# Attention with a key search, experts and a local mixer on one core: small search updates moved to GpSimd, whose instructions then stand in written order

## The chip, the core and the metric

The kernel runs on one core of a Trainium2 chip. A core has five engines that work side by side and wait for each other through semaphores: TensorE (PE in the profile, with its weight loads as PEld), VectorE (DVE), ScalarE (ACT), GpSimd (POOL) and SyncE (SP, here only a queue for DMAs). Each engine takes its instructions in a fixed order: an instruction that waits holds up all that stand behind it on its engine. DMAs move data between DRAM and on-chip memory; SP, ACT and GpSimd issue them, and such an issue is an instruction in that engine's order.

The metric is device time in microseconds (us) of one execution.

## What is computed

Two layers on a batch of 4 images of 32 x 32 tokens with 384 channels. Layer 0 is an attention with a search for important keys, followed by a mixture of 4 experts with the best 2 per token; layer 1 is a local attention over 3 x 3 neighbours and a feed-forward layer. The change touches layer 0:

```python
attn = softmax(einsum('bhnd,bhmd->bhnm', q, k) * scale)
gidx = argmax(einsum('bhnd,hgd->bhng', q, gp), axis=-1)      # 48 groups
q_mean = mean of the q of each group
qmw_t = einsum('bhgd,bhnd->bhgn', q_mean, k)
_, tidx = top_k(qmw_t, 96)                                   # of 1024 keys
col = how often each key was taken, over the groups
attn = attn * row[..., :, None] * col[..., None, :]
attn = attn / (attn.sum(axis=2, keepdims=True) + 1e-08)      # over queries
out = einsum('bhnm,bhmd->bhnd', attn, v) ; x = x + out @ proj_w.T
# experts
probs = softmax(layernorm(x) @ gate_w + gate_b); keep the best two
x = x + sum_e share_e * (gelu(layernorm(x) @ w1[e] + b1[e]) @ w2[e] + b2[e])
```

## The kernel before

**Attention as a pipeline of steps.** There are 48 heads (4 images of 12). A head's 1024 x 1024 scores are done in 4 steps of two 128-key blocks, so there are 192 steps and some more to drain. All instructions are written in one loop, and what is written in a step is spread over time by offsets:

- `scores(u)`: 8 matmuls (L649) into two PSUM buffers; `exps` (L659): two exponentials on ACT that empty them into `e` tiles. The next step's scores need these two buffers back.
- `total`, one step later: 8 matmuls with ones (L667, ps_z) that add up the exponentials by query. After a head's fourth step `gather` copies the sums (ACT, zr, L681) and sends them through DRAM with two DMAs on SP (z_row, zz); `spread` adds and inverts them on DVE (L693, L695) and broadcasts them with two more (r_row, rz).
- `share`, 7 steps after the scores: on DVE, multiplies e by rz (L711, two a step) with a sum by key, and scales v by the inverse (wv, L716, L718).
- `out`, 8 steps after the scores: 8 matmuls (L667, ps_o) of e by wv. After a head's last one `keep` copies the result (po, L731, ACT) and writes it over the head's rows of q: two plain DMAs on SP (L740), then two accumulating DMAs on GpSimd (L738) that add the odd blocks and wait for the plain ones to land.
- Each head works on rows of q and k laid out four times over the partitions (`q4`, `k4`): eight DMAs on GpSimd (L636, L637), written where the head before begins.

**The search** (`topk`) works on tiles of 128 rows of `qmw_t`, 20 tiles in all, at most two at a time. It bisects: ACT counts with a Sign and an accumulator how many of 1024 values are above a bound (L391, into the scratch `junk`), two small DVE instructions on 128 x 1 (L395, L397) make the next bound, and so eight times over; L387 makes the first bound, L401 the edge. Then DVE picks the last candidates (L404, L407 and a chain of small ones to L424), and ACT counts once more (L429). `search()` moves every active search on by one piece and is called twice a step, with `end()` between, so that a Sign and its update stand a step apart. `junk` is the same memory as `below`, which DVE uses in L404.

**Other work in the steps.** A list of units with costs fills TensorE: transposes, q, k and v of the next image, group means, and for the image before, `project` (output projection) with `residue` loading x for it into `o` (one buffer), and `routed`: gate, the best two experts, and 16 indirect DMAs on GpSimd (L1400, two per token tile, four a step) that write token numbers into a table in DRAM by slot.

**Experts.** `experts` runs 35 blocks of 256 slots (three of 128). For each it gathers 2.4 MB of `up` and 2.6 MB of `down` (L1603), slot numbers `ids` (L1617) and token rows `xb` (L1627) with indirect DMAs on GpSimd, double-buffered. The last image's projection, its routing, and `schedule` (which blocks go to which expert, with the running sums `rt_start`) are done beside the first blocks; `add` gathers the two results of a token (`yt`, L1567) when both are there.

**What sets the order.** Attention and experts stand in one region in which the order of PE, DVE, ACT and SP is as written. GpSimd isn't in that list: a scheduler places its instructions, earlier than written where their inputs allow. So the first blocks' weights are issued among the last heads' row loads, and all of a head's eight row loads follow each other.

Of the kernel before, what the change touches and what calls it, by code (L numbers as in the profile page):

```python
# [10 lines left out]
FP = mybir.dt.float32  # L11
BF = mybir.dt.bfloat16
AF = mybir.ActivationFunctionType
ALU = mybir.AluOpType
# [3 lines left out]
P = 128  # L18
B, IMG, C = 4, 32, 384
NTOK = IMG * IMG  # L20
NB = NTOK // P
# [16 lines left out]
FIRST_BOUND, NEAR, SLOPE = 1.65, 92, 0.00366  # L38
# [138 lines left out]
def attention(net, outer, router, x, x1, unsafe, qkv_wT, gpT, proj_wT, proj_w, gate_w, gate_b):  # L177
# [24 lines left out]
    with ExitStack() as ctx:  # L202
# [71 lines left out]
        nc.gpsimd.memset(topped[:, 0, :], 1.0)  # L274
        nc.gpsimd.memset(topped[:, 1, :], float(2 * TOPK - NTOK))
        below = const.tile([P, 512], FP, name="below")
        junk = below.bitcast(mybir.dt.bfloat16)
        fit = const.tile([P, B], FP, name="fit")
        onehot = const.tile([P, B * KC * NB // 2], FP, name="onehot")
        sums = lasting.tile([P, NE], FP, name="sums")  # L280
# [83 lines left out]
        def topk(b, t):  # L364
# [19 lines left out]
            nc.scalar.activation(junk[:n], left[:n], AF.Abs, accum_out=size[:n])  # L384
            yield
            bound = small("tk_bound")
            nc.vector.tensor_scalar(bound[:n], size[:n], -FIRST_BOUND / NTOK, None, ALU.mult)  # L387
            for turn in range(len(DAMP) + 1):
                yield
                over = small("tk_over")  # L390
                nc.scalar.activation(junk[:n], left[:n], AF.Sign, bias=bound[:n], accum_out=over[:n])  # L391
                yield
                if turn == len(DAMP):
                    break
                nc.vector.scalar_tensor_tensor(step[:n], over[:n], float(NTOK - 2 * NEAR), size[:n], ALU.add, ALU.mult)  # L395
                old, bound = bound, small("tk_bound")
                nc.vector.scalar_tensor_tensor(  # L397
                    bound[:n], step[:n], -SLOPE * DAMP[turn] / NTOK, old[:n], ALU.mult, ALU.add
                )
            edge = best[:, 0:1]  # L400
            nc.vector.tensor_scalar(edge[:n], bound[:n], -1.0, None, ALU.mult)  # L401
            for half in range(2):
                cols = slice(half * 512, half * 512 + 512)
                nc.vector.scalar_tensor_tensor(  # L404
# [216 lines left out]
        class Head:  # L621
            def __init__(self, n):
                self.n, self.b, self.h = n, n // NH, n % NH
                self.c, self.j = self.h // 4, self.h % 4
                self.rows = slice(32 * self.j, 32 * self.j + 32)
                self.im = images[self.b]
                assert (self.b, self.c, "qk") in reached

                self.q4 = big.tile([P, 512], FP, name="q4", tag="q4", bufs=2)
                self.k4 = big.tile([P, 512], FP, name="k4", tag="k4", bufs=2)  # L630
                q = self.im["q"][self.c][self.rows, :]
                k = self.im["k"][self.c][self.rows, :].rearrange("p (a e t) -> p a e t", e=2, t=P)
                for r in range(4):
                    rows_ = slice(32 * r, 32 * r + 32)
                    odd, half = divmod(r, 2)
                    nc.gpsimd.dma_start(out=self.q4[rows_, :], in_=q[:, 512 * half : 512 * half + 512])  # L636
                    nc.gpsimd.dma_start(  # L637
                        out=self.k4[rows_, :].rearrange("p (a t) -> p a t", t=P), in_=k[:, :, odd, :]
                    )
                self.es = []  # L640
                self.s = tiny.tile([P, NB], FP, name="s", tag="s")

            def scores(self, u):
                self.ps = []
# [8 lines left out]
                        )  # L653
                    self.ps.append(ps)

            def exps(self):
                for ps in self.ps:
                    e = ep.tile([P, NTOK], FP, name="e", tag="e")
                    nc.scalar.activation(e, ps, AF.Exp, bias=shift, scale=QK_SCALE)  # L659
                    self.es.append(e)  # L660
# [12 lines left out]
            def total(self, u):  # L673
                if u == 0:
                    self.z = ps_z.tile([P, 512], FP, name="ps_z", tag="z")
                self.four(self.z, u, lambda odd: ones)

            def gather(self):

                zr = work.tile([P, 512], FP, name="zr", tag="zr", bufs=1)  # L680
                nc.scalar.copy(zr, self.z)  # L681
                there = rows.tile([4, 512], FP, name="z_row", tag="z_row")
                nc.sync.dma_start(out=there, in_=zr.rearrange("(j r) q -> j r q", r=32)[:, 0, :])
                self.zz = tiny.tile([P, 2, NB], FP, name="zz", tag="zz", bufs=2)
                nc.sync.dma_start(
                    out=self.zz,
                    in_=there.rearrange("j q -> (j q)").rearrange("(e p i) -> p e i", e=2, p=P),
                )
# [68 lines left out]
        def residue(b, t):  # L757
            if late:
                o = late[0].tile([P, C], FP, name="o", tag="o", bufs=2)
            else:  # L760
                o = few.tile([P, C], FP, name="o", tag="o", bufs=1)
            residues[b, t] = o
            r = b * NTOK + t * P
            nc.sync.dma_start(out=o, in_=x[r : r + P, :])
# [81 lines left out]
        def search():  # L846

            for one in list(searching):
                if next(one, 0) == 0:
                    searching.remove(one)  # L850
# [25 lines left out]
        for step in range(-AHEAD, 0):  # L876
# [8 lines left out]
                search()  # L885
            end()
        heads.append(Head(0))
        goal = spent
        for step in range(STEPS + OUT + 2):
            n, u = divmod(step, PAIRS)  # L890
            if n < NHEAD:
                heads[n].scores(u)
            if n < NHEAD:
                heads[n].exps()
            if 0 <= step - OUT < STEPS:
                heads[(step - OUT) // PAIRS].out((step - OUT) % PAIRS)
            if 0 <= step - 1 < STEPS:
                heads[(step - 1) // PAIRS].total((step - 1) % PAIRS)
            if u == 0 and 0 < n <= NHEAD:
                heads[n - 1].gather()  # L900
            if u == 0 and n + 1 < NHEAD:
                heads.append(Head(n + 1))
            if 0 <= step - OUT < STEPS:
                if (step - OUT) % PAIRS == PAIRS - 1:
                    heads[(step - OUT) // PAIRS].keep()
            b, i = divmod(step, PAIRS * NH)
            goal = min(goal + (RAMP if step < 12 else PACE), spent + MOST)
            begin(step)
            if step < 12:
                search()  # L910
                search()
            widen(step)
            o, t = i - OUT - 2, (i - OUT - 2) // 2
            if b and 0 <= o < 2 * NB and o % 2 == 0:
                project(b - 1, t)
            if b and o > 2 * NB:
                next(routing[b - 1], None)
            if b < B:
                for t in {3: [0], 4: [1, 2], 5: [3], 6: [4], 7: [5, 6], 8: [7]}.get(i, []):
                    value(b, t)  # L920
            while spent < goal and prepared():
                pass
            if zeros and step >= 4:
                zeros.pop(0)()
            if 0 <= step - SHARE < STEPS:
                heads[(step - SHARE) // PAIRS].share((step - SHARE) % PAIRS)
            if u == 1 and 0 < n <= NHEAD:
                heads[n - 1].spread()
            if b and 0 <= o + 1 < 2 * NB and o % 2:
                residue(b - 1, t + 1)  # L930
            search()
            end()
            search()
        residue(B - 1, 0)
        assert not ends and not others
        assert pending == [None, None] and begun == len(tiles) and not searching and not zeros
# [304 lines left out]
class Router:  # L1241
# [10 lines left out]
    def __init__(self, net, pool, keep, psum):  # L1252
# [4 lines left out]
        def const(name, shape, dtype=FP):  # L1257
            return pool.tile(shape, dtype, name=f"rt_{name}")
# [38 lines left out]
        nc.gpsimd.memset(self.upto[:, 0, :], 0.0)  # L1297
        self.index = [keep.tile([P, NT], mybir.dt.int32, name=f"index_{n}", tag=f"index_{n}") for n in range(2)]
        self.weight = [keep.tile([P, NT], FP, name=f"weight_{n}", tag=f"weight_{n}") for n in range(2)]
        none = const("none", [P, self.LINE], mybir.dt.int32)  # L1300
        nc.gpsimd.memset(none, 0)
        n = NE * NT
# [10 lines left out]
    def route(self, b, logit, mean, rs):  # L1313
# [82 lines left out]
        for t in range(NB):  # L1396
            if t % 2 == 0:
                yield
            for n in range(2):
                s = nc.gpsimd.indirect_dma_start(  # L1400
                    out=self.net.table, out_offset=bass.IndirectOffsetOnAxis(ap=there[n][:, t : t + 1], axis=0),
                    in_=ids[:, t, :], in_offset=None,
                )
                for o in sent:
                    self.tc.declare_no_dep(s.ins, o, reason="slots of tokens are distinct")
                sent.append(s.ins)
# [920 lines left out]
def metaformer_kernel(  # L2327
# [58 lines left out]
    with ExitStack() as outer:  # L2386
        router = routing(outer)
        eng = mybir.EngineType
        with tc.manual_schedule(engines={eng.PE, eng.DVE, eng.Activation, eng.SP}):
            left = attention(  # L2390
                net, outer, router, x, x1, unsafe, qkv_wT, gpT, proj_wT, proj_w, gate_w, gate_b
            )
            done = experts(net, router, x1, x2, wup, wdown, left)
# [75 lines left out]
```

## Time and profile before

| what | value |
|---|---|
| median of 3 runs (lowest, highest) | 2760.5 us (2757.79, 2776.32) |
| the profiled execution, its span | 2739.55 us, 2737.4 us |
| mean granted clock of TensorE | 0.964 of full |
| busy: PE, DVE, ACT, POOL | 93%, 64%, 46%, 23% |
| first scores of the loop; last ps_o of attention | 80.1 us; 1195.3 us |
| first expert matmul (L1723) | 1198.45 us |
| exponential L659; share L711; Sign L391 | 1107 ns x384; 1275 ns x384; 1151 ns x160 |
| updates L395, L397 | 146 ns, 158 ns, x140 each |
| row loads L636, L637; accumulating stores L738; tables L1400 (on GpSimd) | 512, 657; 885; 1120 ns |

Attention takes about 1100 us, the experts about 985, layer 1 about 557. A profile is one execution; the timed runs lie a little above it. In the answers quoted below, a row of waits gives who waited, for what, and then the sum in us, how many times, and the longest. A row of the timeline gives the start and the length in us, the engine, the source line, the operation, out<-in, and in brackets the idle time before it and what ended it.

### The profile page before, as it was taken

What the parts mean: (1) busy time and instruction counts of PE and PEld (TensorE: products, weight loads), DVE (VectorE), ACT (ScalarE), POOL (GpSimd) and SP (SyncE); (2) the same over time, 40 slices, a digit from 0 to 9 for tenths busy, and PEclk for the clock granted to TensorE, in tenths of its full rate; (3) what the DMA queues carried; (4) which work ended last, traced back from release to release, by engine and by line L of the source; (5) the groups of instructions that cost most, each with busy time, mean ns of one, the idle gap of its engine ahead of it and who ended that gap; (6) DMA issues with size and microseconds to landing.
All of it is one profiled execution on the core that took longest, in us unless ns stands there. A gap on an engine that the chain in (4) does not pass through costs nothing. (4 is left out here: it accounts for less than half of the span.)

```text
span 2737.4 us, 40223 instructions
## 1 busy us (share of the span) xinstructions
PE 2541.4 (93%) x14667; PEld 1549.7 (57%) x14667; DVE 1746.2 (64%) x4490; ACT 1270.0 (46%) x2086; POOL 635.3 (23%) x909
## 2 busy tenths in 40 slices
PE   6979998989899998779999999999999999999988
PEld 3323332333233332248889999999899984555532
DVE  2367768777788778756434454554555468888962
ACT  3768876768677876512122112112111223545455
POOL 2112322252225222613221112222222121210000
PEclk9989999999999998979999999999999999999989
DMA  5133434422332233444574554666566546765532
GB/s 110 38 98 90 105 92 120 106 61 62 83 89 62 62 98 77 138 153 166 214 279 172 202 214 180 219 220 220 197 219 218 213 139 198 224 209 174 181 108 94
DMA packets 189631, 404.14 MB, mean 148 GB/s; under 512 B 83664, under 2 KB 149520, under 8 KB 176368
## 3 DMA queue, kind: packets, MB, share of 16 engines
q0 software_dynamic: 40784, 238.96, 26.5%
q1 hardware_dynamic: 142064, 156.33, 18.3%
q10 hardware_dynamic: 6576, 6.19, 0.8%
q8 instruction: 118, 1.93, 0.3%
q14 instruction: 89, 0.73, 0.1%
HBM read 304.34 MB, written 49.00 MB: 129 GB/s over the span
## 5 line engine op out<-in xcount | busy, mean ns | idle before, releaser
L1728 ACT ACTIVATE h<-ps_h,up 128x256 f32<-128x256 f32 (+1 forms) x420 | 194.8, 464 | 832.2 <-PE ps_h L1723 829.7
L1723 PE MATMUL ps_h<-xbT,up 128*128 128x256 f32 (+1 forms) x2520 | 530.8, 371 | 0.7 <-DVE xbT L1647 0.7
L1723 PEld LDWEIGHTS ps_h<-xbT,up 128*128 128x128 f32 x2520 | 463.3, 191 | 61.7 <-DVE xbT L1647 1.1
L711 DVE CUSTOM_DVE_ANT_0 e<-e,rz,inv 128x1024 f32<-128x1024 f32 x384 | 475.5, 1275 | 17.6 <-DMA rz<-r_row 17.5
L659 ACT ACTIVATE e<-ps_s,ten 128x1024 f32<-128x1024 f32 x384 | 407.1, 1107 | 62.0 <-PE ps_o L667 32.7
L649 PE MATMUL ps_s<-q,k 32*128 32x512 f32 x1536 | 274.3, 663 | 29.1 <-ACT e L659 28.7
L667 PE MATMUL ps_o<-e,wv 128*32 128x512 f32 x1536 | 227.1, 666 | 69.1 <-DVE wv L718 43.9
L636 POOL DMA_DIRECT2D q<-q x192 | 98.2, 512 | 627.9 <-PE ps_s L649 570.5
L667 PE MATMUL ps_z<-e,rt_ones 128*32 128x512 f32 x1536 | 218.8, 642 | 0.0
L391 ACT ACTIVATE below<-tk_left,tk_bound 128x1024 bf16<-128x1024 f32 (+1 forms) x160 | 184.2, 1151 | 63.5 <-DVE tk_bound L397 52.8
L1767 PE MATMUL ps_y<-wsum,hsum 128*128 128x192 f32 x1116 | 197.9, 331 | 10.1 <-DVE hsum L1683 5.9
L1767 PEld LDWEIGHTS ps_y<-wsum,hsum 128*128 128x128 f32 x1116 | 183.7, 192 | 14.3 <-DVE y L1771 7.7
L649 PEld LDWEIGHTS ps_s<-q,k 32*128 32x128 f32 x1536 | 83.0, 188 | 159.6 <-ACT e L659 90.5
L1907 PE MATMUL ps_a<-wa,xnT 128*128 128x486 f32 x384 | 162.3, 572 | 1.8 <-ACT xnT L174 1.8
L1771 DVE TENSOR_TENSOR y<-ps_y,y 128x192 f32<-128x192 f32 x155 | 55.4, 358 | 167.9 <-PE ps_y L1767 164.8
L667 PEld LDWEIGHTS ps_o<-e,wv 128*32 128x32 f32 x1536 | 32.1, 112 | 228.8 <-issue 94.2
L1567 POOL DMA_INDIRECT yt<-yg,index x64 | 78.8, 1232 | 311.4 <-DVE x L1870 148.9
L306 PE MATMUL ps_t<-xnT,wqkv 128*128 128x512 f32 x288 | 136.4, 615 | 3.3 <-ACT xnT L488 2.6
L637 POOL DMA_DIRECT2D k<-k x192 | 126.1, 657 | 9.2 <-issue 6.0
L667 PEld LDWEIGHTS ps_z<-e,rt_ones 128*32 128x32 f32 x1536 | 53.3, 118 | 131.1 <-issue 129.1
L1767 PE MATMUL ps_y<-down,h 128*128 128x192 f32 x744 | 126.0, 326 | 0.0
L1767 PEld LDWEIGHTS ps_y<-down,h 128*128 128x128 f32 x744 | 122.6, 190 | 1.6
(405 smaller groups left out, 3751.1 us busy)
## 6 DMA issues: line engine op xcount, KB each, us to landing
band<-room SPq DMA_DIRECT2D x32, 1560.0 KB
rz<-r_row SPq DMA_DIRECT2D x48, 512.0 KB
yg<-y SPq DMA_DIRECT2D x67, 192.0 KB
q<-q POOLq DMA_DIRECT2D x192, 64.0 KB, 1.9
k<-k POOLq DMA_DIRECT2D x192, 64.0 KB, 2.0
room<-none SPq DMA_DIRECT2D x64, 192.0 KB
x<-x SPq DMA_DIRECT2D x34, 192.0 KB
o<-in_x_dram SPq DMA_DIRECT2D x33, 192.0 KB
```

The lines of the kernel that those rows point to most:

```text
L306: nc.tensor.matmul(ps, lhsT=lhsT(k), rhs=rhs(k), start=k == 0, stop=k == KC - 1)
L391: nc.scalar.activation(junk[:n], left[:n], AF.Sign, bias=bound[:n], accum_out=over[:n])
L636: nc.gpsimd.dma_start(out=self.q4[rows_, :], in_=q[:, 512 * half : 512 * half + 512])
L637: nc.gpsimd.dma_start(out=self.k4[rows_, :].rearrange("p (a t) -> p a t", t=P), in_=k[:, :, odd, :])
L649: nc.tensor.matmul(ps[:, half * 512 : half * 512 + 512], lhsT=self.k4[r, u * P : (u + 1) * P], rhs=self.q4[r, :], start=True, stop=True,)
L659: nc.scalar.activation(e, ps, AF.Exp, bias=shift, scale=QK_SCALE)
L667: nc.tensor.matmul(ps[r : r + 32, :], lhsT=lhsT(odd), rhs=self.es[2 * u + odd][:, half * 512 : half * 512 + 512], start=u == 0, stop=u == ...
L711: nc.vector.tensor_tensor_reduce(self.es[m], self.es[m], self.rz, 1.0, self.im["inv"][:, m, self.h : self.h + 1], ALU.mult, ALU.add, self. ...
L1723: nc.tensor.matmul(ps, lhsT=up[:, o : o + P], rhs=xbT[:, k, :size], start=k == 0, stop=k == KC - 1,)
L1728: nc.scalar.activation(hs[f // 3][:, f % 3, :size], ps, AF.Gelu, bias=up[:, KC * HID + f : KC * HID + f + 1])
L1767: nc.tensor.matmul(ps, lhsT=left[f], rhs=right[:, f, :], start=f == 0, stop=f == HF - 1)
L1907: nc.tensor.matmul(pa[:, :HW_], lhsT=xnTs[i][:, k, :], rhs=wa[:, k, hh * HW_ : (hh + 1) * HW_], start=k == 0, stop=k == KC - 1,)
```

## The change

Six things are changed in attention and one in the region around it.

1. The updates of the search (the first bound, both instructions of each turn, and the edge) are issued on GpSimd. The edge is made with the last bound, ahead of the last Sign.
2. `junk` gets memory of its own; `o` gets two buffers instead of one. The scratch for GpSimd's DMA descriptors is halved, from 8192 to 4096 bytes.
3. GpSimd joins the list of engines whose instructions stand as written. The region spans the experts too.
4. A head's eight row loads become a generator: three, three and two are issued at the ends of the first three steps of the head before.
5. In the step after a head's last one, its last `total` stands right behind the new scores, ahead of `out`; the copy of the sums stands between the two exponentials.
6. Ahead of each table DMA of the routing GpSimd sets a one-column `spacer` to zero.

With the order written, all accumulating stores of the last heads stand ahead of the first expert's weights; `ids`, `up`, `down` and `xb` of a block follow each other; the routing tables stand among loads and updates, four a step; and two memsets of `rt_start`, which stood at the program's start, stand behind the last image's tables and the loads of block 3.

```diff
-        junk = below.bitcast(mybir.dt.bfloat16)
+        junk = const.tile([P, NTOK], BF, name="junk")
...
             bound = small("tk_bound")
-            nc.vector.tensor_scalar(bound[:n], size[:n], -FIRST_BOUND / NTOK, None, ALU.mult)
+            nc.gpsimd.tensor_scalar(bound[:n], size[:n], -FIRST_BOUND / NTOK, None, ALU.mult)
+            edge = best[:, 0:1]
...
-                nc.vector.scalar_tensor_tensor(step[:n], over[:n], float(NTOK - 2 * NEAR), size[:n], ALU.add, ALU.mult)
+                nc.gpsimd.tensor_scalar(step[:n], over[:n], float(NTOK - 2 * NEAR), size[:n], ALU.add, ALU.mult)
                 old, bound = bound, small("tk_bound")
-                nc.vector.scalar_tensor_tensor(
+                nc.gpsimd.tensor_scalar(
                     bound[:n], step[:n], -SLOPE * DAMP[turn] / NTOK, old[:n], ALU.mult, ALU.add
                 )
-            edge = best[:, 0:1]
-            nc.vector.tensor_scalar(edge[:n], bound[:n], -1.0, None, ALU.mult)
+                if turn == len(DAMP) - 1:
+                    nc.gpsimd.tensor_scalar(edge[:n], bound[:n], -1.0, None, ALU.mult)
...
+            def load(self):
...
                     nc.gpsimd.dma_start(out=self.q4[rows_, :], in_=q[:, 512 * half : 512 * half + 512])
+                    yield
                     nc.gpsimd.dma_start(
                         out=self.k4[rows_, :].rearrange("p (a t) -> p a t", t=P), in_=k[:, :, odd, :]
                     )
+                    yield
...
-            def exps(self):
-                for ps in self.ps:
+            def exps(self, which):
+                for ps in self.ps[which]:
...
+            def copy(self):
+
+                self.zr = work.tile([P, 512], FP, name="zr", tag="zr", bufs=1)
+                nc.scalar.copy(self.zr, self.z)
...
-                o = few.tile([P, C], FP, name="o", tag="o", bufs=1)
+                o = few.tile([P, C], FP, name="o", tag="o")
...
             if n < NHEAD:
                 heads[n].scores(u)
+            fresh = u == 0 and 0 < n <= NHEAD
+            if fresh:
+                heads[n - 1].total(PAIRS - 1)
             if n < NHEAD:
-                heads[n].exps()
+                heads[n].exps(slice(0, 1))
+            if fresh:
+                heads[n - 1].copy()
+            if n < NHEAD:
+                heads[n].exps(slice(1, 2))
             if 0 <= step - OUT < STEPS:
                 heads[(step - OUT) // PAIRS].out((step - OUT) % PAIRS)
-            if 0 <= step - 1 < STEPS:
+            if 0 <= step - 1 < STEPS and not fresh:
                 heads[(step - 1) // PAIRS].total((step - 1) % PAIRS)
...
                 heads.append(Head(n + 1))
+                loads = heads[-1].load()
...
             search()
+            for _ in range(3 if u < 3 else 0):
+                next(loads, None)
...
             for n in range(2):
+                nc.gpsimd.memset(self.spacer, 0.0)
                 s = nc.gpsimd.indirect_dma_start(
...
-        with tc.manual_schedule(engines={eng.PE, eng.DVE, eng.Activation, eng.SP}):
+        with tc.manual_schedule(engines={eng.PE, eng.DVE, eng.Activation, eng.SP, eng.Pool}):
...
-    nc = bacc.Bacc("TRN2", target_bir_lowering=False, num_devices=1, dynamic_dma_scratch_size=8192)
+    nc = bacc.Bacc("TRN2", target_bir_lowering=False, num_devices=1, dynamic_dma_scratch_size=4096)
```

More of the change, by code (lines that the diff above doesn't have):

```diff
@@ L630, in __init__ @@
                 self.k4 = big.tile([P, 512], FP, name="k4", tag="k4", bufs=2)
+                self.es = []
+                self.s = tiny.tile([P, NB], FP, name="s", tag="s")
+            def load(self):
                 q = self.im["q"][self.c][self.rows, :]
@@ L639, in __init__ @@
                     )
-                self.es = []
-                self.s = tiny.tile([P, NB], FP, name="s", tag="s")
+                    yield
             def scores(self, u):
@@ L676, in total @@
                 self.four(self.z, u, lambda odd: ones)
+            def copy(self):
+                self.zr = work.tile([P, 512], FP, name="zr", tag="zr", bufs=1)
+                nc.scalar.copy(self.zr, self.z)
             def gather(self):
-                zr = work.tile([P, 512], FP, name="zr", tag="zr", bufs=1)
-                nc.scalar.copy(zr, self.z)
+                zr = self.zr
                 there = rows.tile([4, 512], FP, name="z_row", tag="z_row")
@@ L887, in attention @@
         heads.append(Head(0))
+        for _ in heads[0].load():
+            pass
         goal = spent
@@ L1299, in __init__ @@
         self.weight = [keep.tile([P, NT], FP, name=f"weight_{n}", tag=f"weight_{n}") for n in range(2)]
+        self.spacer = const("spacer", [P, 1])
         none = const("none", [P, self.LINE], mybir.dt.int32)
```

## The prediction

> **What bounds the kernel now.** I read the page first (busy shares and the 40 slices), then five windows cut at the stages, then the waits of PE, ACT and DVE inside attention, then the timeline around one head's end and around the step from attention to the experts.
>
> Windows (stretch, length, busy us of PE, PEld, DVE, ACT, POOL with counts, granted clock, DMA share, GB/s): attention's steady part, its tail, the first experts, the steady experts, layer 1.
>
> ```profile
> 130.00:1060.00 930.00, 851.15 (x5630) 299.34 (x5623) 706.38 (x2085) 687.11 (x1063) 272.49 (x441) 0.95 0.34 87
> 1060.00:1195.00 135.00, 96.23 (x574) 24.62 (x571) 104.08 (x321) 61.92 (x75) 55.21 (x66) 0.82 0.33 94
> 1195.00:1400.00 205.00, 196.06 (x985) 163.16 (x981) 97.93 (x291) 40.86 (x90) 60.04 (x60) 0.97 0.61 224
> 1400.00:2180.00 780.00, 775.45 (x4195) 724.00 (x4195) 403.50 (x734) 147.20 (x311) 165.38 (x156) 1.00 0.57 207
> 2180.00:2737.00 557.00, 522.79 (x2798) 290.08 (x2796) 403.63 (x942) 262.63 (x416) 55.95 (x77) 0.97 0.51 168
> ```
>
> TensorE is the bound everywhere. In the steady part of attention it idles 930 - 851 = 79 us and loses at most (1 - 0.95) x 930 = 46 us to half clock; the tail idles 39 us. The experts have nothing to give: any new wait there is paid in full. So the change can win only out of some 180 us, and can lose anywhere.
>
> Waits in 130 to 1060 (who waited for whom, us, times, longest):
>
> ```profile
> PE ps_s L649 <- ACT e L659: 21.9, 14, 4.1
> PE ps_o L667 <- DVE wv L718: 17.5, 8, 5.0
> PE ps_o L667 <- DVE tk_parts L395: 17.5, 7, 3.9
> PE ps_t L487 <- DVE gate_o L783: 9.0, 5, 3.0
> ACT below L391 <- DVE tk_bound L397: 47.5, 23, 6.2
> ACT tk_left L429 <- DVE tk_parts L424: 30.4, 14, 5.2
> DVE tk_parts L395 <- ACT below L391: 40.7, 28, 3.7
> DVE zall L693 <- DMA zz<-z_row: 36.1, 19, 3.9
> DVE o L782 <- DMA o<-in_x_dram: 13.6, 6, 3.0
> ```
>
> The search and the gather of sums make ACT and DVE wait far more (47.5, 40.7, 36.1) than reaches TensorE (21.9 + 17.5 + 17.5 + 9.0 = 66 us).
>
> **The change, part by part: gains.**
> *Search updates off DVE.* L395 is x140 at 146 ns and L397 x140 at 158 ns: 42 us of DVE work, with L387 and L401 some 44, over about 200 steps 0.2 us a step. DVE no longer queues behind a Sign, and a Sign no longer behind a late share. But of TensorE's 21.9 us on ACT the larger gaps follow the L424 chain, which stays on DVE (PE waits of 3.3, 4.2 and 2.6 us at 366, 425 and 597, each behind an L429 that waited 3.0 to 5.3). I give 9 us here and 6 of the 35 us on wv.
> *junk apart from below:* L404 no longer waits for the Sign's buffer (12.1 us of DVE waits, off TensorE's path); inside those 6 us.
> *o with two buffers:* the load of the next residue no longer waits for the store of the last; of 13.6 us of DVE waits 9.0 reach TensorE. I give 9, and 3 for the half clock after them.
> *Last sums ahead.* In the step after a head, TensorE does the last total before out, and ACT copies zr between the two exponentials. In the step at 624 the copy ran at 627.89; the first exponential and the total both end at about 627.1, so it is some 0.8 us earlier: 19 waits for zz shrink by that, 15 us of DVE, again mostly hidden. The second exponential comes 0.6 us later (the copy's 588 ns); the next scores have about 1.9 us of room (exponentials end 628.0, scores 629.87). Nothing on balance in the steady part.
> *Tail.* There DVE sets the pace, and waits 6.20 + 2.86 + 2.05 + 1.73 us for zz and rz. The first two fall in the burst of the first expert weights (346 GB/s in 1140 to 1150), which moves away (below); the others shrink because the last head's sums need not wait behind out, which itself waited 2.74 us. I give 9 of the 12.8 us.
> Gains: 9 + 6 + 12 + 9 = 36 us.
>
> **Losses: what the written order does to GpSimd's queue.**
> *1. First expert weights behind the last head.* GpSimd's timeline (start, length, what, [idle before, releaser]):
>
> ```profile
> 1141.06 1.03 POOL L1603 DMA_INDIRECT up<-in_wup_dram,rows_w_first  x1 [0.30 <-DVE wv L718]
> 1142.39 0.98 POOL L1603 DMA_INDIRECT down<-in_wdown_dram,rows_w_first  x1 [0.30 <-issue]
> 1148.94 0.95 POOL L1617 DMA_INDIRECT ids<-table,rows_t_first  x1 [0.30 <-issue]
> 1157.77 0.95 POOL L1627 DMA_INDIRECT xb<-x,ids  x1 [7.88 <-DMA ids<-table,rows_t_first]
> 1159.99 1.79 POOL L738 DMA_DIRECT2D q<-po  x2
> ```
>
> Today the scheduler issues up, down, four ids and xb in the middle of the last heads, so the first block starts 3 us after the last ps_o (1195.3 to 1198.45). In written order all eight last accumulating stores (q<-po) stand ahead of up. The last copy of po ends at 1196.0; plus 2.7 us for the landing and 1.6 for two accumulates, up is issued at about 1200.5. From up's issue to xb's took 16.7 us (1141.06 to 1157.77), then about 2.2 for both xb, 2 to land and 2 for norm, transposes and copy: first matmul at about 1223.5. **25 us**, TensorE idle, with nothing else for it: image 3's projections are written inside the first block.
> *2. Updates behind a head's accumulating stores.* One head's end:
>
> ```profile
> 622.70 0.58 ACT L731 COPY po<-ps_o 128x512 f32<-128x512 f32 x1
> 624.76 1.15 ACT L391 ACTIVATE below<-tk_left,tk_bound 128x1024 bf16<-128x1024 f32 x1
> 625.90 2.10 ACT L659 ACTIVATE e<-ps_s,ten 128x1024 f32<-128x1024 f32 x2
> 626.04 1.64 POOL L738 DMA_DIRECT2D q<-po  x2 [1.69 <-ACT below L391]
> ```
>
> The accumulate starts 2.7 us after the copy (its SP stores must land) and takes 1.64. The same step's bound update stands behind it, so the bound is there 2.7 + 1.6 + 0.5 = 4.8 us after the copy. Over the heads from 159 to 983 the next Sign started within 4.8 us of the copy 27 times of 37, typically after 1.5 us: ACT would wait 92 us in all, where it waits 47.5 for bounds now. TensorE: here the Sign moves to 628.2, the exponentials from 625.9 to 629.4, the scores at 629.87 end 1.2 us later. Steps without projection have less room. At 0.9 to 1.2 us for 27 heads: **24 us** (bounds 0, if all hides, and 92).
> *3. Routing's table stores in the same queue.* L1400 is 1120 ns and 0.30 us of gap, four a step, each with a spacer memset (about 0.1 us by the 92 ns memsets): 5.7 us, plus three row loads at 0.58 us, 7.4 us of GpSimd in a step of 5.6. Updates stand behind them; the worst step has the accumulates too. Per image 9 us over four or five steps, images 0 and 1 only (the search is over by image 2): **16 us** (bounds 0 and 30).
> *4. rt_start's memset* leaves GpSimd's start and stands behind 16 tables and xb. Tables ended at 1291.3; behind down (1275.5) and two xb they end near 1301.5, and DVE needs the memset at 1294.5 with hsum queued behind, for which TensorE already waited 5.2 us: **7 us**.
> *5. xb behind down* in the half blocks: issued today some 20 us before down (1345.32 against 1365.94), then right after a 2.6 MB down: **4 us** over two or three blocks.
> *Row loads three per step:* eight a head at 512 and 657 ns, today in one go at the head's start; then three, three and two in the first three steps of the head before. The last two leave a whole step (5.6 us) before the next head's scores and land in 2 us (1.9 and 2.0 in the page): nothing, with that step as cover; without it, 1 to 2 us a head. *Smaller descriptor scratch:* no row of this trace shows a full ring; nothing, at worst some microseconds per weight load, in the experts.
>
> A rule that speaks against the change: the Trainium skill, SBUF — State Buffer, "Who interferes with whom", says that a DVE instruction with two SBUF inputs and a GpSimd one that reads SBUF cannot run together: the later one blocks for the other's whole length. The nearest row is L254, a GpSimd select on 128x1, at 182 ns, but with DVE idle. By the row an update pair costs 0.4 us. By the rule each of the two can meet an L711 (1275 ns, two SBUF inputs, DVE 76% busy here), about 1 us on average for the pair, hidden in most steps and added to part 2's 27: 27 us of ACT, some 9 of TensorE. No row shows it; I take the row and keep the 9 in the range.
>
> **Sum.** +25 +24 +16 +7 +4 -36 = +40 us. Against the profiled execution: 2739.55 + 40 = 2780. That execution lies 0.8% under the median of the runs (2760.5), so for the runs 2760.5 + 40 = **2800 us**.
>
> **Rivals.**
> *A, faster: ACT and DVE freed from each other.* Mechanism: the 47.5 us of ACT and 90 of DVE waits (40.7 + 36.1 + 13.6) drift the three engines apart, and TensorE's 125 us of idling and half clock come from that drift more than from the last named wait. If 75 us of it go, with the tail's 9 and part 2 hidden in ACT's 26% of free time: 2760.5 - 84 + 36 + 10 = 2723. For: long waits come in chains. Against: only 66 us of TensorE's waits are on them. It ends under 2760.5 once the gains pass 46 us with part 2 hidden, and under by one per cent from 73.
> *B, near no change: order hides.* Parts 2 and 3 cost 10 together, the rest as above: 25 + 7 + 4 + 10 - 36 = +10, 2771.
> *C, much slower: GpSimd's queue becomes attention's pace.* Port and queue at the upper ends (part 2 at 50, part 3 at 30, port 9): +89, 2850.
> *D, the order does nothing for sums:* the zr copy still waits for the total on TensorE. Costs only some of the gain: 2805, part of the main case.
>
> **Numbers.** Main case 0.50, A 0.17, B 0.22, C 0.11. Range 2728 to 2848: A's lower half and C's upper half out. One per cent (27 us) is what a measurement can tell from none. Faster 0.16 (A), same 0.24 (B and the low edge of main), slower 0.60.
>
> **What will show it.** First up matmul more than 20 us after the last ps_o, with ids and xb of the first block landing just before (part 1). ACT L392 waiting for GpSimd after po copies, about 3 us each (part 2), longest in the table steps (part 3). DVE's start sums waiting for the memset (part 4). Gone: L391 on tk_bound, DVE on o. I am wrong if the first block starts within 10 us, or if TensorE's idling before 1060 falls by more than 60 us.

## The result and the profile after

The changed kernel takes 2920.0 us (median of 4 runs, 2911.3 to 2930.6) against 2759.1 us for the kernel before on the same chip: ratio 1.0564, 95% interval 1.0532 to 1.0595. The loss is 161 us; 40 were predicted. The profiled execution has a span of 2928.7 us at a mean granted clock of 0.934 (before 0.964).

Cut at the same events as before (first scores, last ps_o, first expert matmul, first matmul of layer 1), the two profiled executions compare as follows, in us:

| stage | before | after | difference |
|---|---|---|---|
| up to the first scores | 80.1 | 83.4 | +3.3 |
| attention, first scores to last ps_o | 1115.2 | 1243.2 | +128.0 |
| gap, last ps_o to first expert matmul | 3.1 | 27.6 | +24.5 |
| experts | 1043.8 | 1075.4 | +31.6 |
| layer 1 to the end | 495.1 | 499.1 | +4.0 |

The differences sum to 191 us, 30 more than the medians differ: the profiled execution of the kernel before lies 20 us under its median, that of the changed kernel 11 us over it. The table also sets right where layer 1 begins in the kernel before: its first matmul is at 2242.3, not at 2180, where the last of the earlier windows is cut, so the experts take 1044 us and layer 1 495.

The windows of the changed kernel at the matching places (stretch, length, busy us of PE, PEld, DVE, ACT, POOL with counts, granted clock, DMA share, GB/s):

```profile
130.00:1185.00 1055.00, 926.16 (x5659) 313.62 (x5661) 682.47 (x1837) 694.16 (x1073) 407.86 (x752) 0.90 0.31 77
1185.00:1327.00 142.00, 100.82 (x562) 24.65 (x552) 95.67 (x283) 59.96 (x72) 57.58 (x97) 0.74 0.23 52
1327.00:1532.00 205.00, 165.28 (x800) 137.37 (x801) 92.10 (x280) 32.81 (x70) 52.91 (x70) 0.89 0.53 195
1532.00:2367.00 835.00, 812.98 (x4382) 751.09 (x4382) 409.01 (x743) 154.81 (x332) 169.05 (x171) 1.00 0.55 206
2367.00:2928.00 561.00, 525.30 (x2791) 290.58 (x2789) 403.70 (x941) 263.01 (x416) 57.27 (x79) 0.96 0.51 167
```

The first row is where most went. For nearly the same matmuls (5659 against 5630) the steady part is 1055 us long instead of 930; TensorE idles 1055 - 926 = 129 us (before 79) and is busy 75 us longer, at a clock of 0.90 instead of 0.95. Its waits in 130 to 1185, and those of ACT, DVE and GpSimd:

```profile
PE ps_s L655 <- ACT e L665: 85.1, 50, 5.7
PE ps_o L673 <- DVE wv L728: 13.8, 5, 4.3
...
ACT junk L392 <- POOL tk_bound L398: 123.5, 30, 7.7
ACT e L665 <- PE ps_o L673: 38.9, 22, 6.9
...
ACT junk L392 <- POOL rt_spacer L1423: 21.4, 2, 10.7
...
DVE zall L703 <- DMA zz<-z_row: 120.0, 33, 8.0
...
POOL q L748 <- DMA q<-po: 341.3, 35, 27.0
```

TensorE now waits for the exponentials 85 us (before 21.9): these stand on ACT behind a Sign that waits for its bound. One head's end in the timeline (start, length, engine, line, [idle before, releaser]):

```profile
622.35 1.15 ACT L392 ACTIVATE junk<-tk_left,tk_bound 64x1024 bf16<-64x1024 f32 x1
...
625.49 0.57 ACT L741 COPY po<-ps_o 128x512 f32<-128x512 f32 x1
...
626.09 1.44 SPq L750 DMA_DIRECT2D q<-po  x2
...
628.81 1.63 POOL L748 DMA_DIRECT2D q<-po  x2 [9.69 <-DMA q<-po]
...
630.08 0.90 POOL L396 TENSOR_SCALAR tk_parts<-tk_over,tk_size 64x1 f32<-64x1 f32 x1
...
631.08 0.30 POOL L398 TENSOR_SCALAR tk_bound<-tk_parts,tk_bound 64x1 f32<-64x1 f32 x1
...
631.41 1.15 ACT L392 ACTIVATE junk<-tk_left,tk_bound 64x1024 bf16<-64x1024 f32 x1 [3.54 <-POOL tk_bound L398]
```

The Sign of 622.35 had its count at 623.6. Nothing but the order kept GpSimd from the update: it sat idle for 9.69 us in front of the accumulating stores, which wait for the plain stores of 626.09 to land. The bound comes 7.8 us after its count, and ACT stands still for 3.54 us with two exponentials behind it.

### The profile page after: what moved, and what is told of

It is laid out like the page before. It is cut to its first block, busy times and chain, and to the rows that moved or that the text cites. A ratio compares the mean times of both kernels' runs of the same rounds, so it can differ in the third digit from the quotient of the medians.

```text
span 2928.7 us, 40456 instructions
## 1 busy us (share of the span) xinstructions
PE 2628.8 (90%) x14667; PEld 1565.6 (53%) x14667; DVE 1709.9 (58%) x4170; ACT 1271.7 (43%) x2086; POOL 776.6 (27%) x1293
## 5 line engine op out<-in xcount | busy, mean ns | idle before, releaser
L665 ACT ACTIVATE e<-ps_s,ten 128x1024 f32<-128x1024 f32 x384 | 414.8, 1111 | 103.3 <-PE ps_o L673 66.1
L655 PE MATMUL ps_s<-q,k 32*128 32x512 f32 x1536 | 323.1, 708 | 99.1 <-ACT e L665 95.9
L673 PE MATMUL ps_o<-e,wv 128*32 128x512 f32 x1536 | 239.6, 700 | 47.2 <-DVE wv L728 45.3
L392 ACT ACTIVATE junk<-tk_left,tk_bound 128x1024 bf16<-128x1024 f32 (+1 forms) x160 | 184.0, 1150 | 176.3 <-POOL tk_bound L398 133.7
L655 PEld LDWEIGHTS ps_s<-q,k 32*128 32x128 f32 x1536 | 93.7, 200 | 259.4 <-ACT e L665 198.3
L673 PE MATMUL ps_z<-e,rt_ones 128*32 128x512 f32 x1536 | 226.6, 664 | 0.0
L748 POOL DMA_DIRECT2D q<-po x96 | 78.9, 918 | 474.6 <-DMA q<-po 417.3
L1627 POOL DMA_INDIRECT up<-in_wup_dram,rows_w_all x31 | 36.6, 1179 | 404.3 <-ACT h L1752 404.0
L396 POOL TENSOR_SCALAR tk_parts<-tk_over,tk_size 128x1 f32<-128x1 f32 (+1 forms) x140 | 75.8, 541 | 207.9 <-ACT junk L392 207.2
```

Of the source, the lines that this page charges most:

```text
L396: nc.gpsimd.tensor_scalar(step[:n], over[:n], float(NTOK - 2 * NEAR), size[:n], ALU.add, ALU.mult)
L655: nc.tensor.matmul(ps[:, half * 512 : half * 512 + 512], lhsT=self.k4[r, u * P : (u + 1) * P], rhs=self.q4[r, :], start=True, stop=True,)
L673: nc.tensor.matmul(ps[r : r + 32, :], lhsT=lhsT(odd), rhs=self.es[2 * u + odd][:, half * 512 : half * 512 + 512], start=u == 0, stop=u == ...
L748: nc.gpsimd.dma_start(out=there, in_=po[r : r + 32, :], accum_op=ALU.add)
```

## The experiments

The versions were timed in four groups (r1 to r4), each beside the kernel before. Its median differs between the groups (2743 to 2759 us), so ratios to it are compared.

| version | median us | ratio | 95% interval |
|---|---|---|---|
| the changed kernel | 2920.0 | 1.0564 | 1.0532 to 1.0595 |
| r1_dve | 2799.7 | 1.0179 | 1.0128 to 1.0229 |
| r1_late | 2798.6 | 1.0162 | 1.0115 to 1.0209 |
| r1_order | 2917.5 | 1.0598 | 1.0548 to 1.0647 |
| r1_loads | 2939.7 | 1.0675 | 1.0624 to 1.0726 |
| r2_written | 2824.9 | 1.0308 | 1.0282 to 1.0334 |
| r2_split | 2753.1 | 1.0034 | 1.0021 to 1.0048 |
| r2_free | 2738.5 | 0.9991 | 0.9977 to 1.0005 |
| r2_dvefree | 2731.0 | 0.9951 | 0.9933 to 0.9969 |
| r3_half | 2842.9 | 1.0311 | 1.0284 to 1.0338 |
| r3_memset | 2791.8 | 1.0126 | 1.0102 to 1.0149 |
| r3_order | 2748.6 | 0.9965 | 0.9949 to 0.9980 |
| r3_bufs | 2745.0 | 0.9954 | 0.9937 to 0.9972 |
| r4_gains | 2731.6 | 0.9947 | 0.9932 to 0.9963 |
| r4_loads | 2729.4 | 0.9951 | 0.9931 to 0.9970 |

Three theories stood at the start: Q, the queue (accumulating stores hold up the updates behind them); P, the price of a small update on GpSimd; S, the new order of sums or of row loads. The first four versions take the changed kernel and undo one thing each.

**r1_dve**, updates back on VectorE:

```diff
-                nc.gpsimd.tensor_scalar(step[:n], over[:n], float(NTOK - 2 * NEAR), size[:n], ALU.add, ALU.mult)
+                nc.vector.scalar_tensor_tensor(step[:n], over[:n], float(NTOK - 2 * NEAR), size[:n], ALU.add, ALU.mult)
...
```

> The changed kernel with the search's small updates back on VectorE, everything else kept. Theory Q (a head's accumulating stores, which wait for another store to land, hold the updates behind them on GpSimd): attention loses all of that, 100 to 130 us of the 160 come back, 2790 to 2820 us. Theory P (a small update takes longer on GpSimd, beside VectorE's two-input instructions above all): the same here, 2790 to 2820. Theory S (the new order of sums, copy and second exponential, or the row loads, lose it): 2890 or more.

**r1_late**, updates still on GpSimd, the stores behind the step's first search call:

```diff
-                            nc.gpsimd.dma_start(out=there, in_=po[r : r + 32, :], accum_op=ALU.add)
+                            added.append((there, po[r : r + 32, :]))
...
             search()
+            accumulate()
             end()
```

> The changed kernel with a head's two accumulating stores issued after the step's first search call instead of before it, so that the update due in that step goes ahead of them; updates stay on GpSimd. Theory Q: most of it comes back, 2800 to 2840 us. Theory P: nothing but a few us, 2900 or more. Theory S: 2900 or more.

Both return some 120 us of the median (2799.7 and 2798.6), 106 and 111 us by the ratios, and attention falls from 1243.2 to 1111.0 and 1110.3 us. r1_late moves a head's two DMA issues past one call and touches nothing else. That settles Q against P and S for this part. The same kind of head's end in r1_late:

```profile
612.77 1.15 ACT L392 ACTIVATE junk<-tk_left,tk_bound 128x1024 bf16<-128x1024 f32 x1
...
614.12 0.26 POOL L396 TENSOR_SCALAR tk_parts<-tk_over,tk_size 128x1 f32<-128x1 f32 x1 [1.77 <-ACT junk L392]
...
614.47 1.31 POOL L398 TENSOR_SCALAR tk_bound<-tk_parts,tk_bound 128x1 f32<-128x1 f32 x1
...
616.05 0.59 ACT L741 COPY po<-ps_o 128x512 f32<-128x512 f32 x1
...
618.10 1.15 ACT L392 ACTIVATE junk<-tk_left,tk_bound 128x1024 bf16<-128x1024 f32 x1
...
619.17 0.85 POOL L757 DMA_DIRECT2D q<-po  x1 [3.39 <-DMA q<-po]
```

The update runs as soon as the count is there, the next Sign does not wait, and the stores still wait 3.39 us for their landing, where nobody is behind them in a hurry.

**r1_order**, the old order of a head's last sums, their copy and the second exponential. 

> The changed kernel with the order of before for a head's last sums, their copy and the second exponential. Theories Q and P: the order was worth something, so 0 to 15 us slower than the changed kernel, 2920 to 2935. Theory S: much of the loss comes back, 2850 or less.

**r1_loads**, all eight row loads where the head begins:

```diff
-                loads = heads[-1].load()
+                for _ in heads[-1].load():
+                    pass
```

> The changed kernel with a head's eight row loads issued together where the head begins, as before, instead of three per step. Theory Q: the loads then stand with their waits ahead of the updates (before's GpSimd waited 500 us for the scores at the first row load), so slower still, 2930 to 3000 us. Theory S: faster, 2880 or less.

r1_order is 2.5 us under the changed kernel by the median and 9 us over it by the ratio, and the intervals overlap: what the order of the sums is worth here, up to some 10 us, can't be told, but it is not the loss. r1_loads is 20 us slower by the median, 31 by the ratio: with GpSimd's order written, the loads in one block are one more thing that the updates stand behind, and in 130 to 1190 ACT waits for bounds 58 times, 181.2 us in all, instead of 30 times. Theory S has fallen.

What remained, 1.0162 in r1_late, was the next question: W, GpSimd's written order among the experts' transfers, or V, the other edits.

**r2_written**, the kernel before with GpSimd added to the list, and the spacer:

```diff
-        with tc.manual_schedule(engines={eng.PE, eng.DVE, eng.Activation, eng.SP}):
+        with tc.manual_schedule(engines={eng.PE, eng.DVE, eng.Activation, eng.SP, eng.Pool}):
```

> The kernel before, with GpSimd's instructions in written order and the small memset ahead of each table store that this order needs; nothing else of the change. Theory W (what is left of the loss, about 44 us, is GpSimd's written order, which puts the experts' transfers behind attention's and in another order among themselves): 2795 to 2815 us. Theory V (what is left comes from the other edits: the smaller descriptor scratch, loads, the buffers): 2755 to 2770.

**r2_split**, r1_late with GpSimd out of the list again for the experts alone:

```diff
+        with tc.manual_schedule(engines={eng.PE, eng.DVE, eng.Activation, eng.SP}):
             done = experts(net, router, x1, x2, wup, wdown, left)
```

> The changed kernel with the accumulating stores behind the first search call, and GpSimd in written order for attention only: in the experts' part the scheduler places its instructions, as before. Theory W: the idle gap ahead of the experts and their slower blocks go, 2745 to 2765 us. Theory V: 2790 to 2800, as without it.

**r2_free**, the changed kernel with GpSimd out of the list throughout. 

> The changed kernel with GpSimd's instructions placed by the scheduler throughout, as before; the updates stay on GpSimd. Theory W with Q: no accumulating store need stand ahead of an update, and the experts' transfers go early: 2740 to 2780 us. Theory V: 2790 or more. If the scheduler leaves the updates behind stores or row loads: 2850 or more.

**r2_dvefree**, the same with the updates on VectorE. 

> The changed kernel with the updates on VectorE and GpSimd placed by the scheduler: what is left of the change is the order of sums, copy and second exponential, the second buffer of the residual rows, the tile of its own for junk, and the row loads. If the prediction's gains for these are real (12 + 9 + some of 6): 2730 to 2740 us. If they were hidden already: 2750 to 2765.

W holds. r2_split brings the gap from 27.7 to 2.1 us and the experts from 1079.6 to 1041.4 us, near the 3.1 and 1043.8 of before. The written order alone (r2_written) costs 3.1%: its gap is 28.0 us, its experts take 1077.2, and its attention is 23 us longer than before. r1_dve, in the same order but with the row loads three per step, the new order of sums and the buffers, has none of these 23; how they divide was not tried. r2_split keeps 1130.4 us of attention against 1110.3 in r1_late: 13 of these 20 us fall between the sums of the last two heads, where the experts' first transfers have come back in among the last stores.

With GpSimd free the updates on it cost little but bring nothing: r2_free is 0.9991, r2_dvefree 0.9951, and the intervals do not meet.

**r3_half**, the stores late for every second head only, asks whether the price adds up by head:

```diff
-                        if odd:
+                        if odd and self.n % 2:
+                            added.append((there, po[r : r + 32, :]))
+                        elif odd:
                             nc.gpsimd.dma_start(out=there, in_=po[r : r + 32, :], accum_op=ALU.add)
...
             search()
+            accumulate()
             end()
```

> The changed kernel with the accumulating stores behind the first search call for every second head only. If each head pays its own delay in full, the 121 us between all heads early (2920) and all late (2799) halve: 2850 to 2870 us. If slack takes up a lone delay: 2830 or less. If any stall drags the rest: 2890 or more.

It came below the middle, 2842.9: half of the heads pay 44 of 121 us (ratios: 1.0311 - 1.0162 = 37% of 1.0564 - 1.0162). How far the copy of a head's sums (zr, on ACT) lags behind r1_late shows the growth over the loop, in us (heads are counted from 0):

| head | 3 | 11 | 19 | 27 | 35 | 43 | 47 |
|---|---|---|---|---|---|---|---|
| the changed kernel | 9.2 | 38.3 | 58.8 | 81.2 | 102.8 | 130.9 | 132.0 |
| r3_half | 4.3 | 17.0 | 26.5 | 32.1 | 38.9 | 49.5 | 50.0 |

There is no single stall: the lag grows by 2.8 us per head on average (132.0 / 47), nearly linearly. After a head without delay some of it is caught up (in r3_half 6.2 us at head 2, 4.3 at head 3).

**r3_memset**, r1_late with the start sums' memsets at the program's start. 

> The changed kernel with all accumulating stores behind the first search call, and the start sums' memsets on GpSimd written once at the program's start instead of among the tables. The prediction's part 4: 7 us less than without it (2799), so 2788 to 2794 us. If the memset hides behind the tables' own lateness: 2796 to 2800.

1.0126 against 1.0162 for r1_late: 10 us by the ratio, 7 by the median, but the intervals overlap, and in the profiles the experts are only 3.6 us shorter (1076.0 against 1079.6). That the memsets cost something is likely; that it is the predicted 7 is not shown.

**r3_order** and **r3_bufs** put one gain each into the kernel before; **r4_gains** has both, **r4_loads** adds the row loads three per step.

> The kernel before with the new order of a head's last sums, their copy and the second exponential, and nothing else. As predicted (9 us in the tail, nothing in the steady part): ratio 0.996 to 0.998. If it is what brings the gain of the version with free GpSimd order and updates on VectorE: 0.995. If it does nothing: 0.999 to 1.001.

> The kernel before with two buffers for the residual rows, memory of its own for junk, and the smaller descriptor scratch that makes room for them. As predicted (12 us, and part of 6): ratio 0.994 to 0.996. If the waits that go were hidden: 0.999 to 1.001. If the smaller scratch stalls GpSimd's transfers: above 1.002.

> The kernel before with the new order of sums, copy and second exponential and with the buffers of the residual rows and of junk (smaller scratch), GpSimd and the updates as before. If the two gains measured alone (0.9965 and 0.9954) add: ratio 0.991 to 0.993. If they remove the same idle time: 0.994 to 0.997.

> The same with the row loads written three per step, GpSimd's instructions still placed by the scheduler. If the loads' new place costs nothing, as predicted: equal to the last within 0.001. If it is what keeps the version with both gains at 0.9951: slower than the last by 0.002 to 0.004.

Each gain alone measures near its size (10 and 13 us), and together they bring 14, not 22. The row loads change nothing that can be measured when the scheduler places them. r4_gains, r4_loads and r2_dvefree, all at 0.995, are the fastest versions seen, ahead of both kernels.

The versions stand in a ladder, one part per rung: 0.9951 (sums, buffers, loads; r4_loads, and r2_dvefree with the spacer) to 0.9991 (updates on GpSimd) to 1.0034 (written order in attention, stores late) to 1.0162 (in the experts too) to 1.0564 (stores ahead of the updates).

## Why the prediction failed in size

**Part 2 is the step that failed.** It said "At 0.9 to 1.2 us for 27 heads: **24 us** (bounds 0, if all hides, and 92)". The mechanism was named and the place was right; the term was 111 to 121 us (the changed kernel against r1_late, by ratio and by median). The 24 is the low end of its own sum (27 x 1.2 is 32), and the 1.2 was one step's delay with all later steps held still. Three things were mis-sized.

- *ACT's waits.* Over 130 to 1330, ACT waits for GpSimd's updates and what stands among them 172.8 us (130.5 + 21.4 + 18.4 + 2.5), in r1_late 26.6: 146 us more, where my upper bound was 92 in all. It counted 27 heads of the schedule as it stood; by the lag of the sums 34 of 47 heads added to the delay.
- *What reaches TensorE.* Set beside r1_late over nearly the same matmuls (130 to 1075: 5696 of them in 945 us, 865.3 busy), the changed kernel idles 128.8 instead of 79.7 us, 49 more.
- *The clock.* The same matmuls are busy 926.2 instead of 865.3 us, 61 more, at a granted clock of 0.90 against 0.96. I had no such term in part 2. The clock that the trace records is either full or half: half for 204.8 us of this stretch, in 30 pieces, and for 81.9 us, in 16 pieces, of r1_late's. At half clock half of the time is lost, and half of the difference of 123 us is 61. In the 3.4 us (the length of the shortest piece) ahead of each of the 30 TensorE was busy for at most 70%, at the median 33%. In windows of 4 us it is plain how a wait pays twice:

```profile
604.00:608.00 4.00, 1.69 (x6) 0.60 (x8) 3.70 (x8) 3.89 (x6) 2.84 (x3) 0.97 0.01 2
608.00:612.00 4.00, 4.00 (x21) 0.60 (x17) 0.37 (x2) 2.61 (x4) 3.37 (x8) 0.60 0.45 85
612.00:616.00 4.00, 4.00 (x22) 2.01 (x18) 3.02 (x5) 1.23 (x4) 0.00 (x0) 1.00 0.43 148
```

In the first TensorE is busy for 1.69 of 4 us, waiting for exponentials behind a late bound; in the second it is fully busy but runs at 0.60. Together 49 + 61 = 110 us is the difference of the two stretches, 1055 - 945.

**Part 1 was right:** predicted 25, measured 24.5 (27.6 - 3.1). From up's issue to xb's it took 16.1 us (16.7 in the prediction), as GpSimd's timeline and TensorE's wait show:

```profile
1329.81 1.56 POOL L748 DMA_DIRECT2D q<-po  x2 [11.97 <-DMA q<-po]
1331.67 1.05 POOL L1627 DMA_INDIRECT up<-in_wup_dram,rows_w_first  x1 [0.30 <-issue]
1333.03 0.98 POOL L1627 DMA_INDIRECT down<-in_wdown_dram,rows_w_first  x1 [0.30 <-issue]
...
1347.73 0.95 POOL L1651 DMA_INDIRECT xb<-x,ids  x1 [8.71 <-DMA ids<-table,rows_t_first]
...
1351.42 0.90 PE L1670 MATMUL ps_t<-ident,xb 128*128 128x128 f32 x3 [24.78 <-DVE xb L1660]
```

r2_split confirms it by taking it away.

**Part 3, the tables: 16 predicted, nothing seen by itself.** In r1_late the tables still stand ahead of the updates, in r1_dve no update stands behind them; attention takes 1110.3 and 1111.0 us, and no Sign of r1_late waits for the spacer. In the changed kernel ACT has two waits of up to 10.7 us on the spacer, where tables and stores come together; no run parts these.

**Parts 4 and 5, and what they missed.** I gave the experts 7 + 4 = 11 us, and they lost 31.6. Counting the up matmuls of r1_late against those of before, the lag grows from 23.5 us at the first to 46.2 at the 600th. Some 9 of these us arise in the fourth block; 7 of them are there in r3_memset too, so they are not the memsets', and their cause stays open. The other 13 arise in the half blocks, where TensorE waits 3.6 and 3.8 us for xb behind down, as part 5 had it, and runs at half clock after each: part 5 was right in kind, and its 4 us too small. The lag stays at 46.2 to the 1090th and reaches 59.3 at the 2472nd. That second rise is not in my list. In the full blocks, GpSimd's timeline in the changed kernel

```profile
2145.01 0.94 POOL L1627 DMA_INDIRECT down<-in_wdown_dram,rows_w_all  x1 [9.24 <-PE ps_y L1791]
2146.26 0.95 POOL L1651 DMA_INDIRECT xb<-x,ids  x1 [0.30 <-issue]
...
2148.78 0.95 POOL L1591 DMA_INDIRECT yt<-yg,index  x1 [0.30 <-issue]
...
2151.28 0.95 POOL L1641 DMA_INDIRECT ids<-table,rows_t_all  x1 [0.30 <-issue]
2165.61 1.32 POOL L1627 DMA_INDIRECT up<-in_wup_dram,rows_w_all  x1 [13.38 <-ACT h L1752]
```

has xb, yt and ids in one burst behind down. In the kernel before xb stands behind down too, but yt comes some 11 us later, and ids 5 us behind up:

```profile
1965.25 0.94 POOL L1603 DMA_INDIRECT down<-in_wdown_dram,rows_w_all  x1 [3.55 <-PE ps_y L1767]
1966.49 0.95 POOL L1627 DMA_INDIRECT xb<-x,ids  x1 [0.30 <-issue]
...
1979.11 1.20 POOL L1567 DMA_INDIRECT yt<-yg,index  x1 [10.42 <-DVE x L1658]
...
1985.85 1.18 POOL L1603 DMA_INDIRECT up<-in_wup_dram,rows_w_all  x1 [3.49 <-ACT h L1728]
```

TensorE's waits on y are 13.2 us after (2000 to 2429) and 3.1 before (1815 to 2242). That the order does it is shown by r2_split, where these waits are 1.2 us (1830 to 2257); which of the moved loads does it was not tried.

**Gains: 36 predicted, 14 measured.** *Tail and sums* (9): 10 alone in the kernel before, but not in the tail, so the size is luck: from the copy of head 43's sums to the last ps_o the profile of r3_order takes 114.6 us and that of r4_gains 108.4, against 105.2 before. What falls is DVE's wait for zz in the steady part (130 to 1060), 36.1 to 22.2 us, near the 15 that I had called mostly hidden. In the changed kernel that wait is 120 (130 to 1185): the copy of the sums stands on ACT behind the delayed Sign. *o's second buffer* (12): 13 together with junk apart and the smaller scratch, but not where I put it: DVE's wait for the residual row is 18.8 us against 13.6 before. The size agrees, the mechanism is not shown. *Search off DVE* (9 + 6): nothing. Over 130 to 1075, Signs wait 46.4 us for VectorE's bounds in r1_dve and 26.6 for GpSimd's in r1_late, but the exponentials' wait behind ps_o rises from 18.0 to 39.5: 64.4 and 66.1 in sum, with r1_dve's two rows first:

```profile
ACT junk L392 <- DVE tk_bound L398: 46.4, 25, 6.0
...
ACT e L665 <- PE ps_o L673: 18.0, 15, 6.9
```

and those of r1_late:

```profile
ACT e L665 <- PE ps_o L673: 39.5, 18, 6.9
...
ACT junk L392 <- POOL tk_bound L398: 26.6, 18, 4.0
```

**The rule weighed.** For a pair of updates I took the row, 0.4 us, and kept in the range what the Trainium skill states (SBUF — State Buffer, "Who interferes with whom": a DVE instruction with two SBUF inputs and a GpSimd one that reads SBUF shut each other out), an estimate of about 1 us. The rule was right about the duration: L396 and L398 average 0.55 + 0.45 = 1.0 us in attention of the changed kernel, and the long ones end with a share on DVE: of 65 that took over 0.4 us and began under a share, 58 ended 0.13 us after it. Two of them:

```profile
604.86 1.27 DVE L721 CUSTOM_DVE_ANT_0 e<-e,rz,inv 128x1024 f32<-128x1024 f32 x1
605.00 1.26 POOL L396 TENSOR_SCALAR tk_parts<-tk_over,tk_size 64x1 f32<-64x1 f32 x1 [1.37 <-ACT junk L392]
...
606.06 1.28 DVE L721 CUSTOM_DVE_ANT_0 e<-e,rz,inv 128x1024 f32<-128x1024 f32 x1
...
606.36 1.11 POOL L398 TENSOR_SCALAR tk_bound<-tk_parts,tk_bound 64x1 f32<-64x1 f32 x1
```

In time it cost nothing that can be seen in written order (r1_late against r1_dve, which differ in the place of the stores too), and with GpSimd free 8 us by the median, 11 by the ratio (r2_free against r2_dvefree), near the 9 that I had kept in reserve.

**Rivals.** C came true, beyond its own number (2850): GpSimd's queue became attention's pace. A fell with the gains, B with part 2. The sums' order does something alone, so D fell; in the changed kernel it can't be told. Of the signs named, the gap over 20 us and the waits of L392 after a po copy were seen, the longest at the tables. A memset of rt_start was waited for, but another one: there are three, and DVE waits 13.2 us for the first (9.9 in r1_late), in attention's tail, where moving it brought nothing (r3_memset: 1110.4 us of attention against 1110.3). At the one that I meant, DVE is idle for 3.2 us in r1_late, and the profile does not name the memset. The Sign's waits for its bound and DVE's wait on o did not go.

## What to carry to other kernels

When a quick step of a loop moves to an engine whose order is written, ask first what stands ahead of it there that waits for a landing: two DMA issues a head, moved past one call, were worth 111 to 121 of 161 us. A wait that recurs in every period is to be charged in every period and with its after-effect on TensorE's clock; the slack seen in one period is largely used up by the next (delayed at every second head, the stores cost 37% of the whole price). An order that a scheduler chose is itself an edit when it is replaced: check each stage that the list covers, not only the one that it was meant for.

## What the runs showed of the hardware

A half-busy stretch of TensorE was followed by reduced clock: busy for 1.69 of 4 us, then a granted clock of 0.60 over the next 4, and over attention that cost 61 us beside 49 of added idling. No long gap was needed: ahead of 23 of the 30 half-clock pieces the longest gap in 6.8 us was 0.65 to 3.3 us. A 128x1 or 64x1 update on GpSimd (L396) took 268 ns at the median and up to 1687 beside VectorE's two-input instructions, where the same on VectorE (L395 in the kernel before) took 153 and at most 161.
